# Layer 0's output projection as seven half products, in a kernel of two cross-attentions

## The chip, the cores and the metric

The kernel runs on one core of a Trainium2 chip, all in float32. The metric is the device time of one execution in microseconds, as the median of several. A profiled execution is traced apart from these; the page's line numbers are those of the kernel before. The engines are named PE (TensorE, matmul), PEld (its weight loads), DVE (VectorE), ACT (ScalarE), POOL (GpSimd) and SP (the queue that issues transfers).

## What is computed

Two cross-attentions follow each other on x (2 x 2048 x 512), both with the same context of 128 rows per batch, 16 heads each:

```python
# layer 0: heads of 64, mask of 0 and 1 per key, max over everything
attn = einsum('bqhd,bkhd->hbqk', x @ Wq + bq, ctx @ Wk + bk) * mask
attn = exp(attn - max(attn)) * mask
attn = attn / (sum(attn, -1) + 1e-15)
out = einsum('hbqk,bkhd->bqhd', attn, ctx @ Wv + bv) @ Wo + bo
y = layernorm(out + x) * gamma + beta
# layer 1: heads of 32, ordinary softmax over the 128 keys
logits = einsum('bhqd,bhkd->bhqk', y @ Wq1.T, ctx @ Wk1.T) / sqrt(32)
ctx1 = softmax(logits) @ (ctx @ Wv1.T)
result = layernorm(y + ctx1 @ Wo1.T + bo1) * gamma1 + beta1
```

## The kernel before

The 4096 tokens are cut into eight blocks t of 512 (four tiles i of 128). The order of work on all five engines is written out by hand; each engine executes its instructions in that order, with semaphores between engines. PSUM is split into two score tiles of two banks each, `sc0` and `sc1`, with one buffer each, two buffers `mm` and two buffers `av` of one bank each.

In the **first phase** (to about 400 us) layer 0's attention is computed. Its query projection already uses seven products of halves instead of eight (`queries_pair`, L332 to L379), with sums of weights (`weight_sums`, L291 to L294) and of tokens (L305 to L316) made on DVE. The unnormalised outputs u (eight rows of 128 features by 512 tokens per block, as four tiles of 128 x 2 x 512) and the denominators go to memory. Denominators are inverted in two halves (`reciprocals0`, L201 and L202).

In the **second phase** `steps(t)` (L872 to L925) lists the steps of round t, for t from -1 to 7. Round t does layer 1's scores of block t, the output projection of layer 1 of block t-1 and layer 0's output projection of block t+1, and fetches block t+2. The steps by their letters:

- F, A, L fetch the residual x (`load_residual`), the reciprocals r and u from memory; N multiplies u by r on POOL (L181, 128x1024); R adds the bias bo0 to the residual on POOL (L190).
- Pr is the output projection of layer 0 for 128 tokens (`project0`, L623: eight matmuls of 512 columns, each two records in the trace, in two parts of four); J adds the residual on DVE (L630); K0 takes mean and variance on DVE (L605 to L614) with a power on POOL (L610, L615); Z normalises on ACT (L638) and makes y = z * gamma + beta on POOL (L640, L641).
- T transposes z on PE (L656) and applies gamma and beta while it leaves PSUM; Q makes layer 1's queries (L674).
- X (`maxima`, L687 to L712) computes the scores of one group of four heads with tokens on partitions, into `sc0` (heads 0 and 1 of the group) and `sc1` (heads 2 and 3). DVE takes the maxima (L693, L707) and scales them (`less`, L700). The exponentials of heads 2 and 3 are eight ACT instructions of 128 columns each with the maximum as bias (L703). For heads 0 and 1, DVE subtracts the maximum (L708) and ACT exponentiates 1024 columns in one instruction (L711). U sums the exponentials on DVE (L717), G inverts the sums (L725). M transposes maxima and shares (L730) and sends them through memory, so that they come back spread over partitions.
- S computes the same scores with keys on partitions (L760) and subtracts the maxima on DVE (L779); P1 exponentiates (L784); V multiplies with the values (L803) and with the shares on DVE (L810).
- E is layer 1's output projection (L825), Y adds y on DVE (L832), I takes the moments, O normalises (L840 on ACT, L843 and L846 on POOL), W stores.

Rounds 1 to 5 are alike. Round 7 ends the work: its softmax divides afterwards (L814, L815), its last normalisation is shared between ACT with POOL and DVE (`norm1_vector`, L855 and L858). A matrix `sel` of minus ones (L110), built at the start, spreads the maxima by matmul in that round alone. The tiles y lie in SBUF from Z to W (12 buffers, `late`).

The steps of such a round, up to Q, as they stand now:

```python
start = [
    (X, t, 0), (J, n, 0), (K0, n, 0), *loads, ..., (Pr, n, 1, 0), (Z, n, 0), ..., (Pr, n, 1, 1), (U, t, 0),
    (X, t, 1), (J, n, 1), (K0, n, 1), (Pr, n, 2, 0), (Z, n, 1), (R, n, 3), (Pr, n, 2, 1), (U, t, 1),
    (X, t, 2), (J, n, 2), (K0, n, 2), (Pr, n, 3, 0), (Z, n, 2), (Pr, n, 3, 1), (U, t, 2), (J, n, 3), *fetches,
    (X, t, 3), (K0, n, 3), (E, l, 0), (Y, l, 0), (U, t, 3), (G, t), (Z, n, 3), (E, l, 1), (Y, l, 1), ...
```

Of the kernel before, what the change touches and what calls it, by code (L numbers as in the profile page):

```python
# [16 lines left out]
P = 128  # L17
TB = 512
NQ = TB // P
EPS_LN = 1e-5  # L20
EPS_SM = 1e-15


@with_exitstack
def two_cross_attentions(
# [79 lines left out]

    sel = const.tile([P, NG, K], F32, tag="sel", name="sel")
    for g in range(NG):
        for r in range(4):
            rows = slice(32 * r, 32 * (r + 1))
            nc.vector.tensor_scalar(  # L110
                sel[rows, g, :], ident[rows, 32 * r + g : 32 * r + g + 1].to_broadcast([32, K]),
                -1.0, None, ALU.mult,
            )
# [7 lines left out]
    wq0s = wide.rearrange("p c m -> p (c m)").rearrange("p (n c m) -> p n c m", n=NG, c=ND)  # L121

# [24 lines left out]
    rows_dram = [dram.tile([2 * NG, 4, TB], F32, tag=f"rows_{t}", name=f"rows_{t}") for t in range(NB)]  # L147
    halves = [range(0, NB // 2), range(NB // 2, NB)]
# [18 lines left out]
    uTs, rs, zs, ys, open0 = {}, {}, {}, {}, {}  # L167
# [37 lines left out]
    with tc.tile_pool(name="w1", bufs=1) as w1, tc.tile_pool(name="a2", bufs=2) as a2, tc.tile_pool(  # L205
# [30 lines left out]
        masks = {0: load_mask(0), 1: load_mask(1)}  # L236
        load_x(0)
        nc.sync.dma_start(wq0s[:, 0], wq0[:, 0])
        bo1s = row(eight, bo1, "bo1", "z")
        load_x(1)  # L240
# [36 lines left out]
        s1 = w1.tile([P, NG, 2, P], F32, tag="s1", name="s1")  # L277
        s2 = w1.tile([P, NG, 2, P], F32, tag="s2", name="s2")
        s4 = w1.tile([P, NG, 2, P], F32, tag="s4", name="s4")
# [177 lines left out]
        bo0s, g0s, b0s = row(const, bo0, "bo0"), row(const, g0, "g0"), row(const, b0, "b0")  # L457
        g1s, b1s = row(const, g1, "g1"), row(const, b1, "b1")
        nc.gpsimd.tensor_tensor(b0s, b0s, bo1s, ALU.add)
# [122 lines left out]
        reciprocals0(0)  # L582
        for g in range(NG):
            fetch_r(0, g)
            normalise(0, g)
# [13 lines left out]
    late = ctx.enter_context(tc.tile_pool(name="late", bufs=12))  # L599
# [18 lines left out]
    def project0(t, i, half):  # L618
        if half == 0:
            open0[t, i] = (av_tile if t == 0 and i < 2 else mm_tile)(f"pso0_{t}_{i}")  # L620
        ps = open0[t, i]
        for n in range(4 * half, 4 * half + 4):
            nc.tensor.matmul(  # L623
                ps, uTs[t, n // 2][:, n % 2, i * P : (i + 1) * P], wo0s[n // 2][:, n % 2, :],
                start=(n == 0), stop=(n == NE - 1),
            )

    def rest0(t, i):
        z = zs[t, i]
        nc.vector.tensor_tensor(z, open0.pop((t, i)), z, ALU.add)  # L630
# [5 lines left out]
    def norm0(t, i):  # L636
        z, (rstd, shift) = zs[t, i]
        nc.scalar.activation(z, z, AF.Identity, bias=shift, scale=rstd)  # L638
        y = late.tile([P, D], F32, tag="y", name=f"y_{t}_{i}")
        nc.gpsimd.tensor_tensor(y, z, g0s, ALU.mult)  # L640
        nc.gpsimd.tensor_tensor(y, y, b0s, ALU.add)  # L641
        zs[t, i], ys[t, i] = z, y
# [37 lines left out]
    def maxima(t, g):  # L680
# [10 lines left out]
        to = tops[t % 2].rearrange("p i (r n) -> p r i n", n=32)[:, :, :, g : g + 1]  # L691
# [7 lines left out]
        less = three.tile([P, 2, NQ], F32, tag="less", name=f"less_{t}_{g}")  # L699
        nc.vector.tensor_scalar_mul(less, to[:, 2:, :], -scaling)  # L700
        for r in range(2, 4):
            for i in range(NQ):
                nc.scalar.activation(  # L703
                    e[:, r, i, :], ps[1][:, r - 2, i, :], AF.Exp, bias=less[:, r - 2, i : i + 1],
                    scale=scaling,
                )
        nc.vector.tensor_reduce(to[:, :2], ps[0], AX.X, ALU.max)  # L707
        nc.vector.tensor_tensor(  # L708
            e[:, :2], ps[0], to[:, :2, :].unsqueeze(3).to_broadcast([P, 2, NQ, K]), ALU.subtract
        )  # L710
        nc.scalar.activation(e[:, :2], e[:, :2], AF.Exp, scale=scaling)  # L711
        open_x[t, g] = e  # L712

    def sums1(t, g):

        to = sums[t % 2].rearrange("p i r n -> p r i n")[:, :, :, g : g + 1]
        nc.vector.tensor_reduce(  # L717
            to.rearrange("p r i o -> p r (i o)"), open_x.pop((t, g)), AX.X, ALU.add
        )
# [3 lines left out]
    def shares1(t):  # L723
        share = tops[t % 2].rearrange("p i (r n) -> p i r n", n=32)[:, :, :, NG : 2 * NG]
        nc.vector.reciprocal(share, sums[t % 2])  # L725

    def turn_maxima(t):
        tr = av_tile(f"trm_{t}")
        for i in range(NQ):
            nc.tensor.transpose(tr[:, i * P : (i + 1) * P], tops[t % 2][:, i, :], ident)  # L730
        tT = two.tile([P, TB], F32, tag="tT", name=f"tT_{t}")
# [21 lines left out]
    def scores1(t, g):  # L753
# [10 lines left out]
        if last:  # L764
            for r in range(4):
                rows = slice(32 * r, 32 * (r + 1))
                nc.tensor.matmul(
                    ps[r // 2][:, r % 2, :], sel[rows, g, :], tTs[t][rows, :], start=False, stop=True
# [17 lines left out]
    def attend1(t, g):  # L786
        b, _ = where(t)
        p1 = probs1.pop((t, g))
        if g == 0:
            ctxs[t] = two.tile([P, NG, TB], F32, tag="ctx", name=f"ctx_{t}")  # L790
# [62 lines left out]
    def norm1_vector(t, i):  # L853
        y, (rstd, mean) = ys[t, i]
        nc.vector.scalar_tensor_tensor(  # L855
            out=y, in0=y, scalar=mean, in1=g1s, op0=ALU.subtract, op1=ALU.mult
        )
        nc.vector.scalar_tensor_tensor(out=y, in0=y, scalar=rstd, in1=b1s, op0=ALU.mult, op1=ALU.add)  # L858

    def store(t, i):  # L860
# [4 lines left out]
    U, G, F, A, D0, J, K0, I = (  # L865
        sums1, shares1, load_residual, fetch_r, reciprocals0, rest0, moments0, moments1
    )
# [148 lines left out]
```

## Time and profile before

| | us |
|---|---|
| median of three runs | 1009.73 |
| lowest, highest | 1008.96, 1010.12 |
| profiled execution | 1010.61 |
| its span in the trace | 1008.8 |
| first phase, to the first L623 | about 399 |
| rounds 2 to 5, from one first X to the next | 72.2 to 72.6 |
| L623, 512 records | 229.4 busy |

Busy times are shares of the span of one engine; several engines work at once, so they don't add up. A line of a timeline gives start, length, engine, line, form and count of merged instructions, and in brackets how long the engine had been idle and what released it. An idle engine costs nothing unless the chain of waits passes through it.

### The profile page before, as it was taken

The numbers are of one execution on the slowest core, as the hardware profiler recorded it, in microseconds if no ns is written. First come the engines' busy times: TensorE is split into PE (matmuls) and PEld (weight loads), VectorE is DVE, ScalarE is ACT, GpSimd is POOL, SyncE is SP. The second block draws the span as 40 slices with busy tenths as digits, with TensorE's granted clock in tenths as the row PEclk, the third lists the DMA queues.
The fourth block names the chain that finished last, engine by engine and source line by source line (L and its number), as shares of the span: only waits on it lengthen the run. The fifth ranks groups of instructions, "written<-read, shape, count | busy, mean of one in ns | idle before, by whom it ended". The sixth has DMA issues, their size and how long they took to land.

```text
span 1008.8 us, 12279 instructions
## 1 busy us (share of the span) xinstructions
PE 985.0 (98%) x4484; PEld 426.3 (42%) x4484; DVE 619.2 (61%) x964; ACT 386.4 (38%) x623; POOL 474.8 (47%) x395
## 2 busy tenths in 40 slices
PE   9999999999999999999999999999999999999995
PEld 5444333333333334474545344344344344344432
DVE  2544645564465452258479578488497496595767
ACT  1133334434334434135344434443344344344250
POOL 0043545443444436772715736636547448344143
PEclk9999999999999999999999999999999999999898
DMA  9314254135234254532622713614523524205111
GB/s 348 121 48 137 58 167 149 53 75 163 54 84 109 81 173 151 172 132 98 229 80 86 285 49 128 255 64 162 211 93 149 185 99 176 78 1 217 37 42 42
DMA packets 50651, 127.12 MB, mean 126 GB/s; under 512 B 9408, under 2 KB 13248, under 8 KB 47008
## 3 DMA queue, kind: packets, MB, share of 16 engines
q1 hardware_dynamic: 48864, 123.72, 36.1%
q0 software_dynamic: 1152, 2.10, 0.8%
q8 instruction: 35, 0.57, 0.3%
q10 hardware_dynamic: 576, 0.53, 0.2%
q14 instruction: 24, 0.20, 0.1%
HBM read 100.15 MB, written 26.18 MB: 125 GB/s over the span
## 4 chain that ended last, share of the span: by engine, by line
PE 88%; DVE 5%; DMA 3%; ACT 2%; issue 1%; POOL 0%; SPq 0%; DVEq 0%; ACTq 0%; POOLq 0%
PE pso L623 21%; PE ps L343 17%; PE pso L825 10%; PE psq_None L674 8%; PE st L391 6%; PE psu L447 5%; PE mx L687 3%; PE s L760 3%; PE den L439 3%; PE u L803 3%; PE psq L674 2%; PE psk L257 2%; PE psq L324 1%; PE psv L269 1%; ACT yT L663 1%
## 5 line engine op out<-in xcount | busy, mean ns | idle before, releaser
L429 POOL TENSOR_TENSOR sm<-sm,mask 128x1024 f32<-128x1024 f32 x64 | 150.2, 2370 | 195.6 <-ACT sm L428 195.6
L623 PE MATMUL pso<-wo,uT 128*128 128x512 f32 x512 | 229.4, 599 | 0.4 <-POOL uT L181 0.4
L610 POOL TENSOR_TENSOR rstd<-rstd,mhalf 128x1 f32<-128x1 f32 x64 | 35.7, 557 | 251.1 <-DVE shift L614 251.1
L623 PEld LDWEIGHTS pso<-wo,uT 128*128 128x128 f32 x512 | 94.3, 190 | 120.8 <-issue 115.3
L825 PE MATMUL pso<-wq,ctx 128*128 128x512 f32 x256 | 115.3, 602 | 0.0
L779 DVE TENSOR_TENSOR p<-s,p 128x1024 f32<-128x1024 f32 x56 | 65.9, 1218 | 62.5 <-PE s L760 55.5
L403 DVE CUSTOM_DVE_ANT_1 sm<-st,mask 128x1024 f32<-128x1024 f32 x64 | 75.8, 1221 | 43.1 <-issue 21.0
L703 ACT ACTIVATE e<-mx,less 128x128 f32<-128x128 f32 x224 | 61.0, 383 | 103.8 <-DVE less L700 103.8
L428 ACT ACTIVATE sm<-sm,ncs 128x1024 f32<-128x1024 f32 x64 | 69.9, 1140 | 73.5 <-DVE ncs L425 73.3
L674 PE MATMUL psq_None<-yT,wq 128*128 128x512 f32 x192 | 88.5, 605 | 1.2 <-ACT yT L663 1.1
L355 DVE TENSOR_TENSOR q<-ps,q 128x512 f32<-128x512 f32 x75 | 51.5, 689 | 56.2 <-PE ps L343 30.0
L343 PE MATMUL ps<-xt,wq 128*128 128x512 f32 x180 | 83.4, 599 | 0.0
L784 ACT ACTIVATE p<-p 128x2048 f32<-128x2048 f32 x28 | 53.5, 1911 | 77.0 <-DVE p L779 45.3
L181 POOL TENSOR_TENSOR uT<-uT,r 128x1024 f32<-128x1024 f32 x32 | 75.1, 2357 | 6.5 <-issue 4.1
L825 PEld LDWEIGHTS pso<-wq,ctx 128*128 128x128 f32 x256 | 47.2, 191 | 57.5 <-issue 51.5
L717 DVE TENSOR_REDUCE sums<-e 128x16 f32<-128x2048 f32 x28 | 63.8, 2278 | 1.1 <-ACT e L711 1.1
L391 PE MATMUL st<-q,k 64*128 64x512 f32 x256 | 63.9, 616 | 0.5 <-DVE q L355 0.5
L447 PE MATMUL psu<-sm,v 128*32 128x512 f32 x512 | 62.6, 598 | 0.0
L693 DVE TENSOR_REDUCE tops<-mx 128x8 f32<-128x1024 f32 x32 | 39.1, 1222 | 31.0 <-PE mx L687 31.0
L343 PE MATMUL ps<-t,s 128*128 128x512 f32 x120 | 56.4, 592 | 0.0
L674 PEld LDWEIGHTS psq_None<-yT,wq 128*128 128x128 f32 x192 | 34.6, 189 | 51.4 <-issue 46.3
L343 PEld LDWEIGHTS ps<-xt,wq 128*128 128x128 f32 x180 | 33.2, 190 | 46.5 <-issue 44.0
(127 smaller groups left out, 1327.2 us busy)
## 6 DMA issues: line engine op xcount, KB each, us to landing
p<-rows SPq DMA_DIRECT2D x28, 1024.0 KB
u<-u SPq DMA_DIRECT2D x32, 512.0 KB
uT<-u SPq DMA_DIRECT2D x32, 512.0 KB
xt<-in_xT_dram SPq DMA_DIRECT2D x16, 512.0 KB
z<-in_x_dram SPq DMA_DIRECT2D x32, 256.0 KB
r<-r SPq DMA_DIRECT2D x32, 256.0 KB
out_dram<-y SPq DMA_DIRECT2D x32, 256.0 KB
r<-rows SPq DMA_DIRECT2D x28, 256.0 KB
```

The source lines that it names most:

```text
L181: nc.gpsimd.tensor_tensor(u, u, r.unsqueeze(1).to_broadcast([P, 2, TB]), ALU.mult)
L343: nc.tensor.matmul(ps, w[:, c, :], x[c] if isinstance(x, tuple) else x[:, c, :], start=(c == 0), stop=(c == 1),)
L391: nc.tensor.matmul(st[n][:, j, :], k0[rows, 2 * g + n, b * K : (b + 1) * K], q[rows, :], start=True, stop=True,)
L403: nc.vector.tensor_tensor_reduce(out=sm, in0=st[n], in1=masks[t].unsqueeze(1).to_broadcast([P, 2, TB]), scale=1.0, scalar=-3.4028234e38, o ...
L428: nc.scalar.activation(s, s, AF.Exp, bias=ncs[:, i + n : i + n + 1])
L429: nc.gpsimd.tensor_tensor(s, s, masks[t].unsqueeze(1).to_broadcast([P, 2, TB]), ALU.mult)
L447: nc.tensor.matmul(ps[32 * j : 32 * (j + 1), :], v0[:, b, d : d + 32], p[j], start=True, stop=True,)
L623: nc.tensor.matmul(ps, uTs[t, n // 2][:, n % 2, i * P : (i + 1) * P], wo0s[n // 2][:, n % 2, :], start=(n == 0), stop=(n == NE - 1),)
L674: nc.tensor.matmul(ps[:, at], wq1s[:, c, g * P : (g + 1) * P], yTs[t][:, c, at], start=(c == 0), stop=(c == ND - 1),)
L717: nc.vector.tensor_reduce(to.rearrange("p r i o -> p r (i o)"), open_x.pop((t, g)), AX.X, ALU.add)
L779: nc.vector.tensor_tensor(p1[:, at], ps[n], p1[:, at], ALU.subtract)
L825: nc.tensor.matmul(ps, ctxs[t][:, g, i * P : (i + 1) * P], wo1s[:, g, :], start=(g == 0), stop=(g == NG - 1),)
```

## The change

A pair of 128-token tiles (i = 0, 1: tiles 2i and 2i+1 of the block) is now projected by seven products of halves. The halves are the two tiles of the pair, the two halves of the 1024 features, and the two halves of the 512 output columns. `output_sums` (SU) makes three sums of u per half block on DVE, of 128x512 each, and one in place (eight instructions a block); three sums of the weights, and one in place, are made once. `product0` (Pd) is one product: four matmuls of 256 columns into half a PSUM bank. The products are combined by DVE adds of 128x256 that read PSUM; the first of a pair is copied by ACT and then added by DVE; POOL adds the combined parts `c2` and `c12` to the residual of the pair's tiles.

The normalised z is stored to memory after Z and fetched back as y (`fetch_y`, YL) into one of 4 buffers, once the output of the block before has left them; POOL applies gamma and beta to it in the next round (`affine0`, GB). `maxima` makes all exponentials in sixteen ACT instructions of 128 columns, straight from both score tiles. `tops`, `sums`, tT and ctx have one buffer instead of two. `sel` is built before round 7 on POOL. The last two tiles' norm reads PSUM instead of y. The steps of all rounds are laid out anew: six of a block's fourteen products stand in the round before, in its second half.

```diff
+    wsums = [const.tile([P, 2 * TB], F32, tag=f"wsum{n}", name=f"wsum{n}") for n in range(3)]
...
+        for q in range(2):
...
+            nc.vector.tensor_tensor(t1, b12, b11, ALU.subtract)
+            nc.vector.tensor_tensor(b12, b22, b12, ALU.subtract)
+            nc.vector.tensor_tensor(t2, b22, t1, ALU.subtract)
+            nc.vector.tensor_tensor(t4, b21, t2, ALU.subtract)
...
-    late = ctx.enter_context(tc.tile_pool(name="late", bufs=12))
+    late = ctx.enter_context(tc.tile_pool(name="late", bufs=LATE))
...
+    def output_sums(t, q):
...
+        (a11, a12), (a21, a22) = halves_u(t, q)
+        s1, s2, s4 = [s[:, 2 * q : 2 * q + 2] for s in sums_u[t]]
+        nc.vector.tensor_tensor(s1, a21, a22, ALU.add)
+        nc.vector.tensor_tensor(a21, a11, a21, ALU.subtract)
+        nc.vector.tensor_tensor(s2, s1, a11, ALU.subtract)
+        nc.vector.tensor_tensor(s4, a12, s2, ALU.subtract)
+
+    def product0(t, i, k):
...
+        ps = (av_tile if k in (2, 7, 4) else mm_tile)(f"pp{k}_{t}_{i}")[:, : TB // 2]
+        for n in range(4):
...
+            nc.tensor.matmul(ps, w, m, start=(n == 0), stop=(n == 3))
...
+        if k == 1:
+            nc.scalar.copy(c12, ps)
+            add(z0[:, lo], z0[:, lo])
+        elif k == 2:
+            add(z0[:, lo], z0[:, lo])
+        elif k == 6:
+            add(c12, c12)
+        elif k == 7:
+            add(c2[:, lo], c12)
+        elif k == 5:
+            add(c2[:, hi], c2[:, lo])
+            add(c12, c12)
+        elif k == 4:
+            add(c2[:, lo], c2[:, lo])
+            nc.gpsimd.tensor_tensor(z1, z1, c2, ALU.add)
+        else:
+            add(c12, c12)
+            nc.gpsimd.tensor_tensor(z0[:, hi], z0[:, hi], c12, ALU.add)
...
         nc.scalar.activation(z, z, AF.Identity, bias=shift, scale=rstd)
+        zs[t, i] = z
+        nc.sync.dma_start(z_dram[t, i], z)
+
+    def fetch_y(t, i):
         y = late.tile([P, D], F32, tag="y", name=f"y_{t}_{i}")
-        nc.gpsimd.tensor_tensor(y, z, g0s, ALU.mult)
-        nc.gpsimd.tensor_tensor(y, y, b0s, ALU.add)
-        zs[t, i], ys[t, i] = z, y
+        nc.sync.dma_start(y, z_dram[t, i])
+        ys[t, i] = y
+
+    def affine0(t, i):
+
+        nc.gpsimd.tensor_tensor(ys[t, i], ys[t, i], g0s, ALU.mult)
+        nc.gpsimd.tensor_tensor(ys[t, i], ys[t, i], b0s, ALU.add)
...
-        nc.vector.tensor_scalar_mul(less, to[:, 2:, :], -scaling)
-        for r in range(2, 4):
+        nc.vector.tensor_scalar_mul(less[:, 2:], to[:, 2:, :], -scaling)
+        nc.vector.tensor_reduce(to[:, :2], ps[0], AX.X, ALU.max)
+        nc.vector.tensor_scalar_mul(less[:, :2], to[:, :2, :], -scaling)
+        for r in (2, 3, 0, 1):
             for i in range(NQ):
                 nc.scalar.activation(
-                    e[:, r, i, :], ps[1][:, r - 2, i, :], AF.Exp, bias=less[:, r - 2, i : i + 1],
+                    e[:, r, i, :], ps[r // 2][:, r % 2, i, :], AF.Exp, bias=less[:, r, i : i + 1],
                     scale=scaling,
                 )
-        nc.vector.tensor_reduce(to[:, :2], ps[0], AX.X, ALU.max)
-        nc.vector.tensor_tensor(
-            e[:, :2], ps[0], to[:, :2, :].unsqueeze(3).to_broadcast([P, 2, NQ, K]), ALU.subtract
-        )
-        nc.scalar.activation(e[:, :2], e[:, :2], AF.Exp, scale=scaling)
...
-            out=y, in0=y, scalar=mean, in1=g1s, op0=ALU.subtract, op1=ALU.mult
+            out=ps, in0=ps, scalar=mean, in1=g1s, op0=ALU.subtract, op1=ALU.mult
         )
-        nc.vector.scalar_tensor_tensor(out=y, in0=y, scalar=rstd, in1=b1s, op0=ALU.mult, op1=ALU.add)
+        nc.vector.scalar_tensor_tensor(out=y, in0=ps, scalar=rstd, in1=b1s, op0=ALU.mult, op1=ALU.add)
...
         if t == -1:
             return [
+                (SU, n, 0), (Pd, n, 0, 1), (SU, n, 1), (Pd, n, 0, 2), *loads, (Pd, n, 0, 6), (Pd, n, 0, 7),
+                (Pd, n, 0, 5), (Pd, n, 0, 4), (Pd, n, 0, 3), (Pd, n, 1, 1), (K0, n, 1), (Pd, n, 1, 2),
+                (K0, n, 0), (Pd, n, 1, 6), (Z, n, 1), (Pd, n, 1, 7), (Z, n, 0), (Pd, n, 1, 5), (Pd, n, 1, 4),
+                (Pd, n, 1, 3), *fetches, (K0, n, 3), (K0, n, 2), (T, n, 0), (Z, n, 3), (Q, n, 0, 0), (Z, n, 2),
+                (Q, n, 1, 0), (Q, n, 2, 0), (R, f, 0), (R, f, 1), (R, f, 2), (R, f, 3), (Q, n, 3, 0), (T, n, 1),
+                (N, f, 0), (N, f, 1), (Q, n, 0, 1), (N, f, 2), (N, f, 3), (Q, n, 1, 1), (SU, f, 0), (SU, f, 1),
+                (D0, 1), (Q, n, 2, 1), (Q, n, 3, 1), (X, n, 0), (Pd, f, 0, 1), (Pd, f, 0, 2), (U, n, 0),
+                (Pd, f, 0, 6), (Pd, f, 0, 7), (Pd, f, 0, 5), (Pd, f, 0, 4),
             ]
...
         start = [
+            (X, t, 0), *loads, *([(V, l, 3)] if t == 1 else []), (Pd, n, 0, 3), (GB, l, 0), (Pd, n, 1, 1),
+            (Pd, n, 1, 2), (U, t, 0), (X, t, 1), (K0, n, 1), (Pd, n, 1, 6), (Pd, n, 1, 7), (GB, l, 1),
+            (Pd, n, 1, 5), (U, t, 1), (X, t, 2), (K0, n, 0), (Z, n, 1), (GB, l, 2), (Pd, n, 1, 4),
+            (Pd, n, 1, 3), *fetches, (Z, n, 0), (E, l, 0), (Y, l, 0), (U, t, 2), (X, t, 3), (K0, n, 3),
+            (GB, l, 3), (E, l, 1), (Y, l, 1), (K0, n, 2), (Z, n, 3), (U, t, 3), (G, t), (E, l, 2), (Y, l, 2),
+            (Z, n, 2),
         ]
...
         return start + [
+            (N, f, 0), (E, l, 3), (Y, l, 3), (M, t), (N, f, 1), (I, l, 0), (T, n), (N, f, 2), (I, l, 1),
+            (Q, n, 0), (N, f, 3), (I, l, 2), (SU, f, 0), (O, l, 0), (Q, n, 1), (SU, f, 1), (I, l, 3), (O, l, 1),
+            (S, t, 0), (P1, t, 0), (W, l, 0), (YL, t, 0), (Q, n, 2), (O, l, 2), (S, t, 1), (P1, t, 1),
+            (V, t, 0), (R, f, 0), (R, f, 1), (W, l, 1), (YL, t, 1), (Q, n, 3), (O, l, 3), (S, t, 2), (P1, t, 2),
+            (V, t, 1), (R, f, 2), (W, l, 2), (YL, t, 2), (Pd, f, 0, 1), (Pd, f, 0, 2), (S, t, 3), (P1, t, 3),
+            (V, t, 2), (R, f, 3), (Pd, f, 0, 6), (Pd, f, 0, 7), (V, t, 3), (W, l, 3), (YL, t, 3),
+            (Pd, f, 0, 5), (Pd, f, 0, 4),
         ]
```

Here n is t+1, f is t+2 and l is t-1.

## The prediction

> **What bounds the kernel now.** I read the page's busy row and clock row first, then the chain of waits, then one steady round engine by engine.
>
> ```profile
> PE 985.0 (98%) x4484; PEld 426.3 (42%) x4484; DVE 619.2 (61%) x964; ACT 386.4 (38%) x623; POOL 474.8 (47%) x395
> PEclk9999999999999999999999999999999999999898
> PE pso L623 21%; PE ps L343 17%; PE pso L825 10%; PE psq_None L674 8%; PE st L391 6%; PE psu L447 5%; PE mx L687 3%; PE s L760 3%; PE den L439 3%; PE u L803 3%; PE psq L674 2%; PE psk L257 2%; PE psq L324 1%; PE psv L269 1%; ACT yT L663 1%
> ```
>
> TensorE sets the time nearly everywhere, and L623, which the change replaces, is the largest step of the chain. The stretches (us; then busy us of PE, PEld, DVE, ACT, POOL) say how little room a steady round of 72.2 us has:
>
> ```profile
> 586.50:658.70 72.20, 71.97 (x343) 31.41 (x341) 52.24 (x75) 30.99 (x55) 40.18 (x40) 1.00 0.41 146
> ```
>
> TensorE in order of time in that round (start us, us, form, count), and two rows of 256-column products from the layer change:
>
> ```profile
> 593.50 1.17 PE L687 MATMUL mx<-k,q 32*128 32x128 f32 x32
> 594.61 7.13 PE L623 MATMUL pso<-wo,uT 128*128 128x512 f32 x16
> 601.67 1.17 PE L687 MATMUL mx<-k,q 32*128 32x128 f32 x32
> ...
> 621.49 0.60 PE L730 MATMUL trm<-ident,tops 128*128 128x128 f32 x4
> ...
> 657.55 1.17 PE L687 MATMUL mx<-k,q 32*128 32x128 f32 x32
> ```
>
> ```profile
> 428.58 7.17 PE L674 MATMUL psq<-yT,wq 128*128 128x256 f32 x32
> 435.59 1.06 PE L656 MATMUL tr<-ident,z 128*128 128x128 f32 x8
> ```
>
> A maxima group (X) starts every 8.17 us, with one token tile's 7.06 us of L623 between; nothing waits. What runs beside it, VectorE and ScalarE in that same stretch:
>
> ```profile
> 588.15 2.18 ACT L703 ACTIVATE e<-mx,less 128x128 f32<-128x128 f32 x8 [7.62 <-DVE less L700]
> 590.52 1.06 ACT L711 ACTIVATE e<-e 128x1024 f32<-128x1024 f32 x1 [0.20 <-DVE e L708]
> ```
>
> ```profile
> 592.20 2.28 DVE L717 TENSOR_REDUCE sums<-e 128x16 f32<-128x2048 f32 x1
> 594.77 1.23 DVE L693 TENSOR_REDUCE tops<-mx 128x8 f32<-128x1024 f32 x1 [0.29 <-PE mx L687]
> ```
>
> The sum of one X (L717) ends 0.3 us before the next maximum: VectorE is nearly full here while TensorE hides it. Lastly a resource that the change leans on:
>
> ```profile
> 1001.74 1.75 DVE L855 SCALAR_TENSOR_TENSOR y<-y,mv,g 128x512 f32<-128x512 f32 x1
> 1003.59 1.57 DVE L858 SCALAR_TENSOR_TENSOR y<-y,rstd,b 128x512 f32<-128x512 f32 x1
> ```
>
> ```profile
> 1001.34 1.60 POOL L843 TENSOR_TENSOR y<-y,g 128x512 f32<-128x512 f32 x1
> 1003.02 1.59 POOL L846 TENSOR_TENSOR y<-y,b 128x512 f32<-128x512 f32 x1
> ```
>
> L855, which reads two SBUF tensors, takes 0.82 us when no long GpSimd instruction is under way and 1.75 here; it ends 0.55 after L843 does, and L846 lasts 1.59 instead of 1.27. The two engines took turns.
>
> **Part 1, the products.** A tile of 512 tokens has four groups of 16 records at 7.06: 28.2 us. Now it has 14 products of 8 records with 256 columns. From 428.58 to 435.59 32 such records take 7.01, 0.219 each, so 1.75 a product and 24.5 a tile: 3.7 saved. The nearest other rows are L543 (3.46 for 16: 24.2, saved 4.0) and the half queries beside waits (3.72 for 16: 26.0, saved 2.2). Taken 3.7, eight tiles, **-30 us if nothing waits**.
>
> **Part 2, the maxima.** VectorE loses L708 (1.22) per X; ScalarE's whole L711 becomes eight more small exponentials, which start 0.25 apart: 16 end 4.2 us after the first. They now read both score tiles, which have one buffer each, so the next X's first matmul waits for the last of them. The sum U waits for them too and stands on VectorE ahead of the next maximum. Walk from X's start at 0, in a round t of 1 to 5: maximum 1.25 to 2.5, `less` 0.2 to 0.3 with its start-up, exponentials 2.8 to 7.1. X1 starts at 7.2 (TensorE was ready at 6.4: 1.1 and three products). Product 1 of the pair is read first by ScalarE's c12 copy, queued behind the 16 exponentials, and VectorE's add of it waits for the copy: 7.4. Then two adds (0.45 and 0.4, as 128x256 at L291), U 2.2 to 10.5, X1's maximum 1.26, `less`, exponentials 12.1 to 16.3. X2 starts at 16.4; TensorE was ready at 13.6. From there U (2.2), maximum, `less` and 16 exponentials make 8.1 us, which X, two products and one 3.5 us projection E just fill: X3 at 24.6. Its exponentials end at 33.3, U3 35.6, reciprocal 36.2, and the transpose of maxima M at 36.4. Before, M stands at 621.49, 36.2 after its X0 (72.2 before 657.55). So this half takes as long as it did, though only eight products (14.0 us) are left in it of the three groups (21.2) before: the saving goes into waits here.
>
> **Part 3, the sums of u.** The other half must hold six products (10.5) where 7.3 us of L623 stood: M 0.4, T 1.9, Q 14.5, S 4.3, V 4.0 and 10.5 make 35.6, the round 72.1 without waits. New on VectorE are eight sums of 128x512 (0.69, as L305) between the moments of layer 1 and the first subtraction of S0 (L779). They read normalised u. GpSimd does that in 2.36 each (L181), behind y's affine part (2 x 1.27) and the powers: its four end at about 36 + 4 x 2.36 + two powers, 46.5. With no clash: last four sums to 49.4, moments 1.1, S0's subtraction to 51.7 for the first tile. S1 is ready on TensorE at 51.4 (Q 39.5 to 43.1, Q 46.7, S0 47.8, Q 51.4), V0 after the exponential (L784, 1.91) 2 us late: round 75. If the sums take turns with GpSimd as L855 did, each can wait for one of its instructions (0.55 to 2.36): sums end at 53 to 54.7, S1 at 55.5 to 57, round 79 to 81. L305 to L316 themselves can't tell, as they met GpSimd for 0.1 us only. Taken 78, **+5.8 in each of five rounds, +29; bounds +2.8 and +8.8**. Behind the sums wait the moments, S0's subtraction, P1 and V0.
>
> [...]
>
> **Part 4, the layer change and rounds -1 and 0.** Before, TensorE runs 401.2 to 427.1 on L623. Now product 2 needs the fourth normalised u (407.6), product 6 eight sums, most of them after it, between three residual adds on GpSimd: begun at 411 to 416, then 12 products (21): transposes at 431 to 437, +4 to +10. The u of tile 1 can be fetched only then; normalising ends near 452, four sums and D0 (1.1 and 3.35) near 459.6, and X0's maximum stands behind them, where VectorE was free at 442.3. X1 starts near 469 instead of 452. Round 0 adds some 2. **+18; bounds +10 and +24.** The weight sums (8 x 0.69) lie in VectorE's 28.7 us of idleness before 417.
>
> **Part 5, the rest.** Round 6 has E3 earlier and no sums: -3. The last norm reads PSUM and one SBUF tensor, four steps near 0.75 instead of the 5.1 from 1000.15: -2. Rows z through memory: eight transfers of 256 KB a round on SP, whose issue rows in this round add up to 34.8 of 72 us; a y is asked for near 55 to 70 of a round and used at 5 to 32 of the next, 15 us of cover; late, it would hold the powers behind it. Half-clock after a wait is left at 0 in the sum:
>
> ```profile
> 944.13 1.93 PE L803 MATMUL u<-p,v 128*32 128x512 f32 x8 [0.49 <-ACT p L784]
> 946.18 2.09 PE L687 MATMUL mx<-k,q 32*128 32x128 f32 x32
> ```
>
> Here, after gaps of 1.0, 0.6 and 0.5, L803 takes 1.93 instead of 1.06 and L687 2.09 instead of 1.17; with the L825 after it (4.40, not 3.70) 2.5 us. Five such rounds would add up to 12.
>
> [...]
>
> **Sum.** 29 + 18 - 3 - 2 = +42, on a profiled execution of 1010.6 (span 1008.8 and 1.8 around it), 0.9 above the median of the three runs. From the median: about 1050. Low ends 14 + 10 - 5 = +19: 1029; high ends 44 + 24 - 5 = +63, and something of the clock: 1076.
>
> **Rivals.** (a) The waits are hidden and TensorE stays the bound: -30, -2, +4 for the first tile: 982. For it: PE 98%, X2 to X3 and M are just filled; against it: U waits for sixteen exponentials and stands before the next maximum. It decides if X1 to X2 takes 6.4 and not 9.2. (b) The sums don't clash and the layer change costs its least; a round 72 to 74: 1010 to 1025. For it: GpSimd is idle for a good part of a round. [...]
>
> **Chances.** Forecast 0.52, (b) 0.20 (0.04 of it within 0.2%, about what a measurement here can tell from no change), (c) 0.09, (a) 0.19. Faster 0.19, same 0.04, slower 0.77. The likeliest case's own range is 1029 to 1076; reaching into (b) and (c): 1006 to 1078.
>
> **What would show it.** X1 to X2 at 9.2 and X2 to X3 at 8.1, with X waiting for ScalarE; L717's successor idle for `e`; u's sums longer than 0.69 where GpSimd runs; S1 waiting for VectorE; the second reciprocal (L202) ending after the first X's matmuls. Wrong if products cost over 1.9, if X follows X within 6.5, or if GpSimd's normalising comes much earlier than 46 in a round.

## The result, and the profile after

| | before | after |
|---|---|---|
| median of four runs (lowest to highest) | 1009.5 us (1008.96 to 1010.12) | 1093.55 us (1086.73 to 1097.34) |
| ratio, 95% interval | | 1.0825 [1.0769, 1.0880] |
| profiled execution, span | 1010.6, 1008.8 | 1086.73, 1085.0 |
| mean granted clock of the span | 0.993 | 0.957 |
| start of X0 of rounds 0, 1, 6 | 444.05, 511.78, 874.65 | 453.31, 538.05, 947.33 |
| rounds 1 to 5, mean from X0 to X0 | 72.6 | 81.9 |

The change makes the kernel 8% slower. The forecast was 1050 us with a range up to 1078, so the direction was right and the size was not. The page of the changed kernel (busy time and share, granted clock in 40 slices, the chain that ended last):

```profile
PE 993.3 (92%) x4868; PEld 513.9 (47%) x4868; DVE 681.3 (63%) x1116; ACT 418.2 (39%) x835; POOL 517.6 (48%) x442
PEclk9999999999999997989999999899899999899989
PE 69%; DVE 12%; ACT 7%; POOL 6%; issue 2%; DMA 2%; SPq 0%; POOLq 0%; ACTq 0%; DVEq 0%
```

The chain's row before:

```profile
PE 88%; DVE 5%; DMA 3%; ACT 2%; issue 1%; POOL 0%; SPq 0%; DVEq 0%; ACTq 0%; POOLq 0%
```

TensorE had 98% of the span before and has 92% now. In the chain it fell from 88% to 69%; what came instead is VectorE, ScalarE and GpSimd, that is to say waits for them. The clock row has eights and a seven from the layer change on, where there were nines up to the last slices.

One steady round (stretch; length, busy us of PE, PEld, DVE, ACT, POOL, granted clock, DMA share, GB/s):

```profile
703.11:785.76 82.65, 74.58 (x389) 42.90 (x388) 59.74 (x95) 35.28 (x85) 44.55 (x44) 0.94 0.42 153
```

Before, the same row read 72.20 long and 71.97 busy at a clock of 1.00. Here 8.1 us are idle, and the work, which should have become less, takes 74.6 us at 0.94. TensorE in that round, in order of time (start, duration, what it waited for):

```profile
710.20 1.17 PE L756 MATMUL mx<-k,q 32*128 32x128 f32 x32 [0.53 <-ACT e L774]
...
719.41 2.09 PE L756 MATMUL mx<-k,q 32*128 32x128 f32 x32 [2.66 <-ACT e L774]
721.43 2.69 PE L661 MATMUL pp<-wsum,uT 128*128 128x256 f32 x8
...
740.91 0.66 PE L796 MATMUL trm<-ident,tops 128*128 128x128 f32 x4
...
759.92 3.21 PE L826 MATMUL s<-q,k 32*128 32x512 f32 x8 [4.54 <-DVE p L845]
763.05 1.94 PE L869 MATMUL u<-p,v 128*32 128x512 f32 x8
764.92 4.83 PE L743 MATMUL psq_None<-yT,wq 128*128 128x512 f32 x8
769.68 1.14 PE L826 MATMUL s<-q,k 32*128 32x512 f32 x8
```

Two waits matter: X2 for ScalarE's exponentials (2.66) and S1 for VectorE (4.54). What follows each is slow: X2 takes 2.09 instead of 1.17, V0 1.94 instead of 1.07, Q3 4.83 instead of 3.70. The next round has the same wait without the slowness:

```profile
802.34 1.17 PE L756 MATMUL mx<-k,q 32*128 32x128 f32 x32 [2.66 <-ACT e L774]
```

What VectorE did meanwhile, in the round from 703.11, and GpSimd beside it:

```profile
747.91 0.69 DVE L641 TENSOR_TENSOR usum<-uT,uT 128x512 f32<-128x512 f32 x1 [1.12 <-POOL uT L179]
748.64 2.87 DVE L642 TENSOR_TENSOR uT<-uT 128x512 f32<-128x512 f32 x1
751.42 0.68 DVE L643 TENSOR_TENSOR usum<-usum,uT 128x512 f32<-128x512 f32 x1
752.14 1.80 DVE L644 TENSOR_TENSOR usum<-uT,usum 128x512 f32<-128x512 f32 x1
753.86 1.75 DVE L641 TENSOR_TENSOR usum<-uT,uT 128x512 f32<-128x512 f32 x1
...
758.65 2.34 DVE L845 TENSOR_TENSOR p<-s,p 128x1024 f32<-128x1024 f32 x2
```

```profile
748.61 2.34 POOL L179 TENSOR_TENSOR uT<-uT,r 128x1024 f32<-128x1024 f32 x1
750.91 0.99 POOL L620 TENSOR_TENSOR rstd<-rstd,mhalf 128x1 f32<-128x1 f32 x1
...
752.12 1.26 POOL L909 TENSOR_TENSOR y<-y,g 128x512 f32<-128x512 f32 x1
753.47 1.59 POOL L912 TENSOR_TENSOR y<-y,b 128x512 f32<-128x512 f32 x1
```

The reader should see the eight sums of u in front of S0's subtraction. Three of them take 1.75 to 2.87 us instead of 0.69, and they are the ones that start while GpSimd is in its normalising (L179) or in layer 1's affine part (L909, L912); each ends 0.55 or 0.56 us after the GpSimd instruction that it met. GpSimd's own instructions there are longer too: a power takes 0.99 instead of 0.55, L912 1.59 instead of 1.27. S0's subtraction starts at 758.65, though its scores were there at 751.7, and S1 waits for it.

By the profiled execution the 76.2 us are 26.3 up to X(1,0), 46.4 in rounds 1 to 5, and 3.5 behind them. The other three runs of the changed kernel were 5.6 to 10.6 us longer at lower clocks (0.947 to 0.950). Since its runs scatter like this, the experiments are read by their rounds first.

### The profile page after: what moved, and what is told of

The parts are those of the page before. It is cut to its first block, busy times and chain, and to the rows that moved or that the text cites. A ratio compares the mean times of both kernels' runs of the same rounds, so it can differ in the third digit from the quotient of the medians.

```text
span 1085.0 us, 13697 instructions
## 1 busy us (share of the span) xinstructions
PE 993.3 (92%) x4868; PEld 513.9 (47%) x4868; DVE 681.3 (63%) x1116; ACT 418.2 (39%) x835; POOL 517.6 (48%) x442
## 4 chain that ended last, share of the span: by engine, by line
PE 69%; DVE 12%; ACT 7%; POOL 6%; issue 2%; DMA 2%; SPq 0%; POOLq 0%; ACTq 0%; DVEq 0%
PE ps L341 17%; PE pp L661 13%; ACT e L774 6%; PE st L389 6%; PE psu L445 5%; PE pso L891 5%; PE s L826 4%; PE psq_None L743 3%; PE u L869 3%; PE den L437 3%; POOL uT L179 3%; PE mx L756 2%; DVE sums L783 2%; DVE tops L762 2%; DVE uT L642 2%
## 5 line engine op out<-in xcount | busy, mean ns | idle before, releaser
L774 ACT ACTIVATE e<-mx,less 128x128 f32<-128x128 f32 x448 | 118.9, 416 | 145.3 <-DVE less L769 117.2
L661 PE MATMUL pp<-wo,uT 128*128 128x256 f32 x384 | 93.3, 393 | 4.1 <-POOL uT L179 4.1
L850 ACT ACTIVATE p<-p 128x2048 f32<-128x2048 f32 x28 | 53.5, 1911 | 98.1 <-issue 82.3
L661 PEld LDWEIGHTS pp<-wo,uT 128*128 128x128 f32 x384 | 74.2, 196 | 21.7 <-POOL uT L179 6.5
L661 PE MATMUL pp<-wsum,usum 128*128 128x256 f32 x256 | 66.6, 404 | 12.7 <-DVE z L672 8.3
L179 POOL TENSOR_TENSOR uT<-uT,r 128x1024 f32<-128x1024 f32 x32 | 75.6, 2378 | 5.2 <-DVE wsum L587 3.3
L688 POOL TENSOR_TENSOR z<-z,c 128x512 f32<-128x512 f32 x16 | 20.3, 1267 | 116.8 <-DVE c L672 116.8
L826 PE MATMUL s<-q,k 32*128 32x512 f32 x256 | 49.0, 729 | 26.3 <-DVE p L845 22.7
L661 PEld LDWEIGHTS pp<-wsum,usum 128*128 128x128 f32 x256 | 49.0, 199 | 31.7 <-issue 14.3
```

Of the source, the lines that this page charges most:

```text
L179: nc.gpsimd.tensor_tensor(u, u, r.unsqueeze(1).to_broadcast([P, 2, TB]), ALU.mult)
L661: nc.tensor.matmul(ps, w, m, start=(n == 0), stop=(n == 3))
L774: nc.scalar.activation(e[:, r, i, :], ps[r // 2][:, r % 2, i, :], AF.Exp, bias=less[:, r, i : i + 1], scale=scaling,)
L826: nc.tensor.matmul(ps[r // 2][:, r % 2, :], k1[rows, g, b * K : (b + 1) * K], q1s[t][rows, g, :], start=True, stop=not last,)
```

## The experiments

Each is the changed kernel with one edit, except e7 (the kernel before with one edit) and the last two. "Rounds" is the mean of rounds 1 to 5 from X0 to X0, 81.9 in the changed kernel.

| run | median us | ratio to before, 95% interval | rounds | X(1,0) |
|---|---|---|---|---|
| e1_no_sums | 1037.1 | 1.0274 [1.0254, 1.0293] | 73.8 | 528.7 |
| e2_exps_old | 1089.1 | 1.0780 [1.0764, 1.0796] | 82.3 | 538.8 |
| e4_no_memory | 1089.9 | 1.0790 [1.0765, 1.0815] | 81.8 | 540.0 |
| e7_before_exps | 1013.4 | 1.0042 [1.0028, 1.0057] | 73.2 | 513.0 |
| e9_no_normalise | 1073.0 | 1.0622 [1.0606, 1.0638] | 79.2 | 537.8 |
| e3_fill | 1093.7 | 1.0836 [1.0806, 1.0866] | 82.3 | 538.6 |
| e3b_fill5 | 1075.8 | 1.0652 [1.0636, 1.0668] | 79.8 | 538.6 |
| e5_q3_first | 1073.4 | 1.0628 [1.0612, 1.0644] | 78.6 | 539.2 |
| e6_layer_change | 1085.3 | 1.0740 [1.0714, 1.0766] | 82.7 | 533.2 |
| e13_quiet_sums | 1076.0 | 1.0651 [1.0635, 1.0667] | 79.4 | 536.9 |
| e12_new_order | 1029.9 | 1.0193 [1.0169, 1.0218] | 74.3 | 519.9 |
| e14_clear_queues | 1006.3 | 0.9964 [0.9953, 0.9975] | 71.5 | 514.8 |

**Without the sums of u.**

```diff
 def output_sums(t, q):
+    if t > 0:
+        sums_u[t] = sums_u[0]
+        return
     if q == 0:
```

> Left out: the sums of u of blocks 1 to 7 (block 0's stand in for them, and the in-place difference isn't made), so layer 0's projection of those blocks is another. Theory (waits from VectorE's order): the 4.5 us wait of S1 in a steady round and the half clock behind it (about 3 us) go, and so does the 8.3 us wait for VectorE after the first X of layer 1; 5 x 7.5 + 8 = about 45 us less than the changed kernel, 1040 to 1058, with rounds of 74 to 76. Rival (the rows z through memory, or the products themselves): rounds stay at 80 to 83 and the time within 10 us of the changed kernel's 1093.

S1 waits for nothing any more and runs in 1.14; rounds take 72.4 to 75.7, and X1 follows X0 of the layer change without the 8.3 us. The sums, with all that follows from them, carry 50 us of the profiled span and 56 of the median. Whether it is their work or their place, this run can't tell. What is left above the kernel before, 27 us, is what the other parts cost, less what the products save.

**Before's maxima.** The diff puts back one exponential of 128x1024 behind a subtraction of VectorE:

```diff
-        for r in (2, 3, 0, 1):
+        for r in range(2, 4):
...
+        nc.vector.tensor_tensor(
+            e[:, :2], ps[0], to[:, :2, :].unsqueeze(3).to_broadcast([P, 2, NQ, K]), ALU.subtract
+        )
+        nc.scalar.activation(e[:, :2], e[:, :2], AF.Exp, scale=scaling)
```

> The maxima as before the change (VectorE subtracts half of the scores, one exponential of 128x1024 for them), all else as changed. Theory (the chain maximum, sixteen exponentials, sum sets X1 to X3): the score tiles come free about 2 us earlier and each sum starts 1 us earlier, so X0 to M is 32 us instead of 36.5 to 37.8; 4 us in each of seven rounds, 1062 to 1080. Rival (X1 to X3 are set by the products and VectorE's adds, and the exponentials' place doesn't matter): M stays near +36, the time 1088 to 1100, for VectorE gets 1.2 us more work in each X.

The theory missed. X1 and X2 do come earlier (6.5 and 13.6 us after X0, not 7.1 and 16.3), but M comes at +36.5, no earlier than in the changed kernel's round from 785.76, for VectorE has 1.2 us more in each X (33.6 us busy up to M instead of 29.1): the projections E between X3 and M wait for it (0.46 and 1.60). The changed kernel's other rounds have M at +37.9, for half rate follows X2 or X1 is late. What is won on these is lost again behind M: S1 waits 4.97 instead of 4.54, and the half rate there lasts 10.2 us in four of five rounds, where it lasted 6.8 in four of five. The half of a round up to M is full on two engines, and taking from one gives to the other.

**The exponentials alone,** in the kernel before (the same lines the other way round):

> The kernel before with the changed maxima alone: both halves by sixteen exponentials of ScalarE, read from the scores. Theory (the chain of 8.1 us from X to X just fits a round whose X start every 8.17 us, and nothing is taken from that cover): 1008 to 1018. Rival (sixteen exponentials cost some us in each round whatever lies beside them): 4 us in seven rounds, 1035 or more.

Where X follows X every 8.2 us in any case, the sixteen exponentials cost 0.4%, some 0.7 us in a round.

**Rows z not through memory.**

```diff
-        nc.sync.dma_start(z_dram[t, i], z)
-        nc.sync.dma_start(y, z_dram[t, i])
+        nc.sync.dma_start(y, x[b, q0 + i * P : q0 + (i + 1) * P, :])
```

> Left out: the store of the normalised rows z; y is fetched from the rows of x instead, so layer 1's residual is another. Half of the added transfers go, and no fetch of y stands behind a store. Theory (waits from the order on VectorE, GpSimd and ScalarE; the rows through memory are hidden): within 5 us of the changed kernel, 1086 to 1100, rounds 80 to 83. Rival (the transfers or SyncE's queue hold the rounds): rounds fall below 78, time below 1070.

Every round has its length to the tenth (81.6, 83.5, 82.6, 80.0, 81.6). The store, and a fetch that has to wait for it, cost nothing here; the fetches themselves stayed.

**Without GpSimd's normalising.**

```diff
 def normalise(t, g):
     u, r = uTs[t, g], rs.pop((t, g))
+    if t > 1:
+        return
```

> Left out: GpSimd's normalising of u for blocks 2 to 7, so their layer 0 is another; VectorE's eight sums a round stay. Theory (the sums cost through the turns that they take with GpSimd and through waiting for its last normalised u): the sums take 0.69 each, S0's subtraction comes 4 to 5 us earlier, S1 doesn't wait, rounds 73 to 76, time 1045 to 1060. Rival (VectorE's own 5.5 us of sums in front of S0's subtraction is what costs, whoever runs beside them): rounds stay above 79, time above 1075.

Between the two. Six sums take 0.69; two still take 1.73 and 1.75, beside layer 1's affine part. S0's subtraction comes 5 us earlier in its round, and S1's wait falls from 4.54 to 1.08. But the round falls by 2.7 only. TensorE there, and the granted clock (eighth value of a row: stretch, length, five engines, clock):

```profile
748.21 2.72 PE L828 MATMUL s<-q,k 32*128 32x512 f32 x8 [1.08 <-DVE p L847]
751.34 1.94 PE L871 MATMUL u<-p,v 128*32 128x512 f32 x8 [0.40 <-ACT p L852]
```

```profile
749.00:750.00 1.00, 0.99 (x6) 0.30 (x4) 0.90 (x2) 0.63 (x1) 0.92 (x2) 0.94 0.26 100
750.00:751.00 1.00, 0.93 (x4) 0.00 (x0) 0.64 (x2) 1.00 (x1) 0.44 (x1) 0.50 0.26 100
...
755.00:756.00 1.00, 1.00 (x3) 0.41 (x2) 0.00 (x0) 0.00 (x0) 1.00 (x2) 0.50 0.25 98
756.00:757.00 1.00, 1.00 (x3) 0.46 (x2) 0.00 (x0) 0.00 (x0) 1.00 (x2) 0.64 0.27 104
757.00:758.00 1.00, 1.00 (x3) 0.38 (x2) 0.00 (x0) 0.00 (x0) 0.61 (x1) 1.00 0.26 100
```

A wait of 1.08 us with two short ones behind it is followed by 6.8 us at half rate, from 749.9 to 756.7 (a mean of 0.94 in the first of these rows is 0.12 us at 0.50, one of 0.64 in the fourth 0.72). Half the rate for 6.8 us is 3.4 us lost, more than the wait. Such rows of the changed kernel put its own stretch at 760.4 to 767.2, as long, behind a wait of 4.5, and a shorter one of 3.4 us at X2.

**A filler in the wait.** Matmuls of `ident` by `wo1`, into a tile that nothing reads, between Q2 and S1: ten of them, then five.

```diff
+    ps = av_tile(f"fill_{t}")
+    for _ in range(10):
+        nc.tensor.matmul(ps, ident, wo1s[:, 0, :], start=True, stop=True)
```

> Added: ten 128x512 matmuls on TensorE (4.4 us) between Q2 and S1 of rounds 1 to 5, into a tile that nothing reads, where TensorE waits 4.5 us. Theory (the half clock behind the wait is a cost of its own): S1 takes 1.2 to 2.2 instead of 3.2, V0 1.07 instead of 1.94, Q3 3.7 instead of 4.8; of the 4 us about 2 lie on the path, for V0 waits for the exponential anyway; 1078 to 1087, rounds 79 to 80.5. Rival (the slow S1, V0 and Q3 aren't the clock but waits for tiles): same durations, time 1090 or more.

Ten took 8.75 us, for each makes two records of 0.44; the sizing was off by two. S1 starts 4.2 us later than it could, and still the rounds are as long as in the changed kernel: with the clock at full rate, V0 1.07 and Q3 3.70, those 4.2 us came back.

> The filler again with half as many matmuls: five of 128x512, which issue ten records or 4.4 us, between Q2 and S1 of rounds 1 to 5 (with ten they took 8.75 us, 4.2 too many, and the round grew by nothing). Theory (the wait is followed by some 6 us at half rate, a cost of its own): S1 1.2 to 1.8, V0 1.07, Q3 3.7, the granted clock 1.00 there, rounds 79 to 80.5, time 1078 to 1086. Rival (what the half rate takes is hidden by the wait of V0 for its exponential): rounds at 81.5 or more, time 1088 or more.

```profile
669.83 4.46 PE L940 MATMUL fill<-wq,ident 128*128 128x512 f32 x10
674.54 2.26 PE L826 MATMUL s<-q,k 32*128 32x512 f32 x8 [0.25 <-DVE p L845]
677.66 1.07 PE L869 MATMUL u<-p,v 128*32 128x512 f32 x8 [0.86 <-ACT p L850]
```

The granted clock of that round is 1.00 and it takes 79.0. Work that nobody needs makes the kernel faster: by 2.1 us in a round and 10 in the profiled span, 18 by the medians. The half rate behind the wait is a cost of its own. Not all of it belongs to S1's wait: of the changed kernel's rounds 1 to 5, three have half rate at X2 or just behind it as well (X2 to X3 9.8 or 9.9 us instead of 8.2), here only one. The changed kernel's round from 785.76, with the half rate at S1 alone, takes 80.0, against 79.0 here.

**Q3 in the wait.** Order alone:

```diff
-  (S, t, 0), (P1, t, 0), ..., (Q, n, 2), (O, l, 2), (S, t, 1), (P1, t, 1),
-  (V, t, 0), ..., (Q, n, 3), (O, l, 3), (S, t, 2), (P1, t, 2),
+  (S, t, 0), ..., (Q, n, 2), (Q, n, 3), (P1, t, 0), (O, l, 2), (S, t, 1), (P1, t, 1),
+  (V, t, 0), ..., (O, l, 3), (S, t, 2), (P1, t, 2),
```

> Only the order in rounds 1 to 5 is another: Q3 before S1 (and the first exponential P1 behind Q3's copy on ScalarE); no work is removed. Theory (TensorE waits for VectorE with work at hand that doesn't depend on it): the wait of S1 falls from 4.5 to about 1 us, S2 and S3 follow 5 us earlier, and with the wait goes the half clock: rounds 76 to 78, time 1062 to 1076. Rival (S1's lateness sets the rest of the round whatever TensorE does meanwhile: P1, V0, S2 in a chain): rounds stay at 80 to 82, time 1085 to 1095.

Within the expected time, a little above the expected rounds. The wait is 1.10, but the half rate stays (S1 2.84, V0 1.93, S2 2.09 in the round from 695.83), and rounds fall by 3.2, not by 5.

**The layer change.**

```diff
-  (K0, n, 2), (T, n, 0), ..., (R, f, 0), (R, f, 1), (R, f, 2), (R, f, 3), ..., (T, n, 1),
-  (N, f, 0), ..., (SU, f, 0), (SU, f, 1), (D0, 1),
+  (K0, n, 2), (D0, 1), (T, n, 0), ..., (T, n, 1),
+  (N, f, 0), ..., (R, f, 0), (R, f, 1), (R, f, 2), (R, f, 3), ..., (SU, f, 0), (SU, f, 1),
```

> Only the order in round -1 is another: the second reciprocal (3.35 us) before the transposes instead of behind the sums of u of block 1, and the residual adds of block 1 behind its normalising on GpSimd. Theory (X0's maximum on VectorE stands behind both): the maximum starts 4 to 6 us earlier, the wait behind X0 falls from 8.3 to 2 to 4 us, time 1085 to 1090 (5 less). Rival (the wait comes from the late u alone): under 1 us less.

X0's maximum starts at 458.0 instead of 463.3, the wait behind X0 is 3.5 instead of 8.3, and X(1,0) comes 4.8 us earlier. The sums are still slow (five take 1.6 to 2.8): now they meet the residual adds as well.

**The sums where GpSimd is idle.** Normalising earlier, sums before layer 1's moments; nothing left out:

```diff
+  (N, f, 0), (N, f, 1), (X, t, 3), (K0, n, 3), ...
-  (N, f, 0), (E, l, 3), (Y, l, 3), (M, t), (N, f, 1), (I, l, 0), (T, n), (N, f, 2), (I, l, 1),
-  (Q, n, 0), (N, f, 3), (I, l, 2), (SU, f, 0), (O, l, 0), (Q, n, 1), (SU, f, 1), ...
+  (E, l, 3), (Y, l, 3), (M, t), (N, f, 2), (N, f, 3), (T, n), (Q, n, 0), (SU, f, 0), (Q, n, 1), (SU, f, 1),
+  (I, l, 0), (O, l, 0), (I, l, 1), (O, l, 1), (S, t, 0), ...
```

> Only the order in rounds 1 to 5 is another: the first two normalisings of u before the fourth maxima and the other two before layer 1's moments on GpSimd, the sums of u on VectorE before those moments (so that GpSimd has nothing to run beside them), and u fetched ahead of the store of z. All the work stays. Theory (it is the clash and the late u that cost, not VectorE's own time in sums): the sums take 0.69 each, S1 doesn't wait, rounds 73 to 76 as without sums (73.8), time 1048 to 1065. Rival (VectorE has too much to do in this half): rounds 78 or more, time 1073 or more.

```profile
742.73 0.69 DVE L642 TENSOR_TENSOR uT<-uT 128x512 f32<-128x512 f32 x1
743.34 0.68 DVE L643 TENSOR_TENSOR usum<-usum,uT 128x512 f32<-128x512 f32 x1
744.05 0.69 DVE L644 TENSOR_TENSOR usum<-uT,usum 128x512 f32<-128x512 f32 x1
```

```profile
752.65 1.14 PE L826 MATMUL s<-q,k 32*128 32x512 f32 x8
756.33 1.06 PE L869 MATMUL u<-p,v 128*32 128x512 f32 x8 [2.54 <-ACT p L850]
```

The sums are as fast as expected, S1 doesn't wait, and yet the round is 78.4. One part is a wait that has moved on: V0 waits 2.54 for the exponential P1. P1 stands on ScalarE behind layer 1's whitening, which waits 3.5 us for a power on GpSimd, which stands behind the affine part of the tile before. The other part stands ahead of M:

```profile
714.96 2.09 PE L756 MATMUL mx<-k,q 32*128 32x128 f32 x32 [2.66 <-ACT e L774]
716.98 3.78 PE L661 MATMUL pp<-wsum,uT 128*128 128x256 f32 x8
```

X2 and the products behind it run at half rate for 6.8 us in rounds 2 to 5, and X3 comes at +27.6, where the kernel with five fillers, at full rate there, has +24.5. Without these 3.1 us the round would be some 75, an estimate, and the first bet would hold. So by time the rival was nearer, but not for its reason: the clash is removed, and a queue and the clock take its place.

**All places at once.** Block 0 by whole products again with the weight sums behind it, products 5 and 4 of a pair behind the next X0, Q3 before S1, E3 before M in round 6; the same diff changes the lists of rounds -1, 0 and 6; its core in a steady round is the head of the list. A second version puts right what the trace of the first showed.

```diff
-  (X, t, 0), *loads, ..., (Pd, n, 0, 3), (GB, l, 0), (Pd, n, 1, 1), (Pd, n, 1, 2), (U, t, 0), (X, t, 1),
+  (X, t, 0), *loads, ..., (Pd, n, 0, 5), (Pd, n, 0, 4), (GB, l, 0), (Pd, n, 1, 1), (U, t, 0), (X, t, 1),
+  (Pd, n, 0, 3), (Pd, n, 1, 2), ...
```

> All of it together, and more: block 0 of layer 0 by whole products as before the change (no sums ahead of it; the weight sums after it), the second reciprocal early, u normalised early and the sums before the moments, Q3 before S1, the last two products of a pair moved from the end of a round behind the next X0, so that X1 to X2 has 8.7 us of products instead of 5.3, and E3 before M in round 6. Theory (the changed arithmetic is cheaper and only its places cost): rounds 67.5 to 71, X(1,0) near 508, time 985 to 1008. Rival (VectorE, or the half rate after waits that stay, holds the rounds at 72.2 or more): 1010 to 1040.

The rival was nearer: 74 us a round and 1030 us. On VectorE of that run:

```profile
624.61 2.10 DVE L785 TENSOR_SCALAR less<-tops 128x8 f32<-128x8 f32 x1
626.62 1.21 DVE L786 TENSOR_REDUCE tops<-mx 128x8 f32<-128x1024 f32 x1
627.87 1.15 DVE L787 TENSOR_SCALAR less<-tops 128x8 f32<-128x8 f32 x1
```

`less`, eight numbers a partition and 0.17 us elsewhere, takes 2.10 and 1.15 beside the normalising that this order puts there (624.32 to 629.0). Sixteen exponentials stand behind it. The second version puts the normalising behind `less`, P1 ahead of Q2's copy, residual adds ahead of the product that needs them:

```diff
-  (U, t, 2), (N, f, 0), (N, f, 1), (X, t, 3), (K0, n, 3), (GB, l, 3), (E, l, 1), (Y, l, 1), (K0, n, 2),
+  (U, t, 2), (X, t, 3), (K0, n, 3), (N, f, 0), (E, l, 1), (Y, l, 1), (K0, n, 2), (N, f, 1),
...
-  (I, l, 0), (S, t, 0), (O, l, 0), (I, l, 1), (O, l, 1), (W, l, 0), (YL, t, 0), (Q, n, 2), (Q, n, 3),
-  (P1, t, 0), (I, l, 2), (I, l, 3), (O, l, 2), (S, t, 1), (V, t, 0), (R, f, 0), (R, f, 1), (Pd, f, 0, 1),
+  (I, l, 0), (S, t, 0), (O, l, 0), (P1, t, 0), (I, l, 1), (Q, n, 2), (R, f, 0), (R, f, 1), (O, l, 1),
+  (W, l, 0), (YL, t, 0), (Q, n, 3), (I, l, 2), (I, l, 3), (O, l, 2), (S, t, 1), (V, t, 0), (Pd, f, 0, 1),
```

> As the last (the new order), with what its trace showed put right: GpSimd's first normalising behind the small `less` operations of the fourth maxima (they took 2.10 and 1.15 us instead of 0.17 beside it), P1 of the first tile ahead of Q2's copy and of layer 1's whitening on ScalarE, residual adds before the product that needs them, block 0's weight sums on both sides of the transposes' copies, the second reciprocal in an idle stretch of round 0, round 0's first transposes before its fourth maxima, and layer 1's affine rows of the last round one round earlier. Theory (waits from places alone): M at +37.5 instead of 39.3, V0 without its wait of 1.4 us, rounds 70 to 71.5; X(1,0) at 508 to 513; 990 to 1008. Rival (VectorE's work, some 60 us of a round, can't be laid without waits): rounds 72.5 or more, 1012 to 1030.

```profile
PE 964.6 (96%) x4820; PEld 492.1 (49%) x4820; DVE 657.0 (65%) x1096; ACT 417.3 (42%) x833; POOL 511.2 (51%) x438
```

```profile
588.28:659.24 70.96, 68.84 (x393) 40.65 (x389) 56.63 (x95) 35.45 (x85) 43.93 (x44) 1.00 0.52 182
```

Rounds 2 to 5 take 71.0 and M stands at +37.3, as expected; X(1,0) at 514.8 is 2 us later than expected. The time is 1006.3 us, a ratio of 0.9964 [0.9953, 0.9975]: 0.4% below the kernel before, little but clear of the interval. The row is the one to set beside the first of this part: the same arithmetic in a round with 2.1 us idle instead of 8.1, and 68.8 busy at 1.00 instead of 74.6 at 0.94.

## Why the prediction was right in direction and wrong in size

**Part 1, products: right in kind, a little high.** At full clock a steady round's TensorE work falls from 71.97 to 68.84 (e14), 3.1 us a tile, where 3.7 was said. The 30 us never became time in the changed kernel, as forecast.

**Part 2, the chain of maxima: right.** X1, X2, X3 and M were put at 7.2, 16.4, 24.6 and 36.4 after X0. The round from 785.76, with full rate behind X2's wait, has them at 7.4, 16.6, 24.8 and 36.5. In four of the rounds 1 to 6 half rate set in at X2 or just behind it, which puts M 1.4 later, at +37.9; the first has X1 at 9.5 and M there too. Rival (a) needed 6.4 from X1 to X2; it is 9.2.

**Part 3, the sums: the mechanism was right, the value taken was not.** Full turn-taking put the end of the sums at +53 to +54.7, S1 at +55.5 to +57 and the round at 79 to 81. They ended at +54.5 and S1 started at +56.8, in a round whose M was 1.4 late. I took 78, the middle between clash and no clash, though the only row of the old trace (L855, 1.75 instead of 0.82) spoke for the clash. The term was 29 for five rounds and measured 46.4. Some 12 of this are the clock's, as the next paragraph shows, so that the waits alone come near 34, inside the bounds of 14 and 44.

**The clock, put at 0 in the sum: the step that failed.** The row shown in part 5 (2.5 us behind small gaps) named it, with 12 us for five rounds. It was left out of the sum all the same, on an estimate of mine that no run shows. That is what failed: X2's wait of 2.66 was followed by half rate in four of the rounds 2 to 6. The fill runs show it as a cost of its own, 10 us of the profiled span. The trace's clock records have eight stretches at half rate in rounds 1 to 5, 47.8 us together, where the kernel before had none. The filled kernel's rounds without such a stretch take 79.0 (the first 80.7); against them the five rounds are 12.5 us longer, an estimate of what the clock cost there. For the high end's "something of the clock" no run shows a figure; these 12.5 us stand in its place. The round from 703.11 has three times 3.41 us of half rate, two behind S1's wait and one at X2: 5.1 us lost, half of 10.2.

The clock reached further than the steady rounds. Ahead of X(1,0) TensorE worked without waiting through some 12 us at half rate, so about 6 of them were lost; in round 6 two stretches, at X2 and behind M, cost some 3 (both estimates, half of the time at half rate). And the three longer runs of the changed kernel, which put the median 7 us above the profiled run, have spans 5.5 to 10.6 us longer, while their span times (1 - clock), the time lost at half rate, is 8 to 11 us more. Of the 43 us by which 1093.55 exceeds 1050 some 28 are thus the clock's, by these estimates.

**Part 4, the layer change: 18 said, 26.3 measured, some 6 of it the clock's.** Transposes at 436 lay in the forecast's 431 to 437. Then X0's maximum started at 463.3 and not at 459.6: the last normalising ended at 454.1 (452 said) and the first sum took 2.82 beside it. The products behind X0 waited 8.28 for VectorE and the next two ran at half rate (3.78 and 2.02 instead of 1.99 and 1.89), so X1 stood at 475.4, not 469. The late `D0` and sums were named; e6 gives 4.8 us back at X(1,0) by their order.

**Part 5: -5 said, +3.5 measured.** The end behind the last projection is 2 us shorter, as said. Round 6, put at 3 us shorter, is 1.5 longer: M waits 3.5 us for the reciprocal of the last sums, with E3 still behind it, which then runs at half rate (5.29 instead of 3.70). In e12, with E3 before M, that round takes 64.9 instead of 67.8. Round 7 lost 4 that were not in the sum. ScalarE of the changed kernel there:

```profile
1038.91 0.81 ACT L906 ACTIVATE y<-y,shift,rstd 128x512 f32<-128x512 f32 x1 [7.65 <-POOL shift L625]
1043.21 0.81 ACT L906 ACTIVATE y<-y,shift,rstd 128x512 f32<-128x512 f32 x1 [3.49 <-POOL shift L625]
1043.93 1.92 ACT L843 ACTIVATE p<-s 128x1024 f32<-128x1024 f32 x2
```

The exponentials of the last S0 stand behind a whitening, and that behind a power on GpSimd, whose queue now also holds layer 0's affine rows (two instructions of 1.27 a tile) in the last round. S1 waits 3.6 us instead of 1.2. I had counted those rows in steady rounds only. With them moved a round earlier, among other things (e14), X(7,0) to the end takes 63.4 us instead of 69.8.

**Rows through memory** at no cost: right as far as e4 tested it, for the store and the order behind it.

Together: 46.4 instead of 29, 26.3 instead of 18, 3.5 instead of -5, and 7 us by which the median of the runs lies above the profiled one. The first three make the 76.2 us of the profiled execution; its high end was put at 63 and something of the clock.

The clash with GpSimd is not one of the sums alone (0.69 alone, 1.75 to 2.87 beside it). The 128x8 `less`, which reads a single tensor, was held too (0.17 against 2.10, e12). Which of VectorE's instructions are held, and why, was not isolated.

## What to carry to other kernels

A wait on the engine that sets the time costs more than its length if the clock falls behind it (in e9 6.8 us at half rate, 3.4 lost, behind a wait of 1.08): price it by what such gaps show in the same trace, and put independent work into it. Where instructions of two engines were seen to lengthen each other (here a sum from 0.69 to 2.87 beside L179, L912 from 1.27 to 1.59 beside a sum), place them in different stretches, small instructions at the head of a chain above all (`less` from 0.17 to 2.10). When arithmetic is saved on the bounding engine by giving more to others, the order of all queues has to be laid out anew before the saving shows: here nearly the same work (block 0's products aside) took 1094 and 1006 us.

## What was not expected of the hardware

The half-rate stretches here do not follow from the length of the wait. Behind S1 of the changed kernel it lasted 6.8 us after a wait of 4.5; in e9 6.8 us after one of 1.08; in e13 V0 waited 2.54 and the clock stayed at 1.00; X2's 2.66 were followed by 3.4 us of it in the round from 703.11, by 6.8 in e13 and by none in the round from 785.76.

The clock records show what the stretches went with. In the changed kernel's trace all fifteen begin whole multiples of 3.41 us apart (637.53, 675.08, 719.45 and 760.41 are 11, 13 and 12 times 3.41 apart), and those that are over before the trace ends last one to five times 3.41. I divide the time at full rate from 420 us on into pieces of 3.41 us, laid on these beginnings, and count TensorE's busy time in each. All 12 pieces with under 1.4 us of work were followed by half rate, none of the 142 with over 2.6 was, and of the 18 between 2 were. X2's wait of 2.66 fell into one piece in the round from 703.11, with 0.75 us of work, and half rate followed; in the round from 785.76 it lay across two, with 1.7 and 2.4 us of work, and none did. In e9 TensorE was busy for 2.3 of the 3.41 us ahead of the drop at 749.9. What decides between 1.4 and 2.6 was not isolated.
